# First scan's convolution: four taps on VectorE and GpSimd, or four products with diagonal matrices on TensorE

## The chip, the cores and the metric

The kernel runs on one core of a Trainium2 chip. The metric is the device time of one execution in microseconds; three runs of the kernel before gave 3540.46, 3543.61 and 3543.66 us, a median of 3543.61. All data are float32 unless a line says otherwise.

## The reference, cut to what matters

The input `x` is 32 sequences of 256 tokens with 256 channels. A recurrent block (state space scan) is followed by two transformer layers; the result is added to `x`. Only the front of the recurrent block matters here:

```
xr, gate = split(x @ W_in.T, 2)                 # 512 channels each
xr = xr + t_emb[:, None, :]
xc = conv1d(xr, W_conv, causal, 4 taps, one filter per channel) + b_conv
xc = silu(xc)
xn = layernorm(xc)                              # over the 512 channels
Bm, Cm, dt = split(xn @ W_xproj.T, 3)
h[t] = clip(h[t-1] * Ad[t] + Bd[t] * xn[t], -10, 10)   # scan over 256 tokens
y[t] = Cm[t] . h[t] + D * xn[t];  out = (y * silu(gate)) @ W_out.T
```

The convolution works on each channel by itself: output token t is the sum over k = 0..3 of weight k times input token t - 3 + k. With channels on the 128 partitions, multiplying by one weight per partition is the same as a matrix product with a diagonal 128x128 matrix.

## The kernel before, in words

The 32 sequences are four groups of `GB` = 8. `group_scan(g)` writes the scan of one group: 256 steps in `NCH` = 8 chunks of `CH` = 32 tokens. The 512 inner channels are `NC_` = 4 blocks of 128. For the first group the flag `alone` is true: no transformer work of an earlier group runs beside it. The other groups' scans run beside the transformer layers of the group ahead of them.

All work of a scan is put into numbered slots by `at(slot, function, arguments)`, one slot per step of the recurrence, counted from the scan's first step. `scan_slots` emits the slots in order; a slot's agenda of part 1 comes ahead of its part 2. The framework then orders each engine's instructions itself, by a modelled readiness with the order of emission as the priority (so ScalarE's `tanh` of slot -19 is run ahead of the SiLU of slot -36), allots buffers and sets the semaphores. On the chip every engine follows its fixed order. SyncE issues nearly all loads; its queue is in order too.

Ahead of a chunk that starts at slot s0, block `ch` goes through:

- `project` (slot s0-40+2ch, L401): TensorE multiplies the inputs `xg` by `w_in_sb` into a bank, `ps_in`.
- `conv_in` (s0-38+2ch): GpSimd puts the last three tokens of the chunk before into `xr` (L473, from `carry`); VectorE adds the condition and writes the 32 new tokens of the 8 sequences (L474); GpSimd makes the first tap and the bias, `acc = xr * w0 + b` (L480), and saves the last three tokens (L485). `xr` and `acc` have two buffers each.
- `conv_taps` (s0-37+2ch): VectorE adds three more taps into `acc` (L491).
- `conv_th` (s0-36+2ch): for the first group ScalarE makes `xc = silu(acc)` (L501); for other groups a tanh is used and VectorE finishes in `conv_out` (L511).

Then `raw_sums` (L520, TensorE, slot s0-27) and `norm_turn` (L550, transposes into `tp_x`, s0-26 and s0-22) read `xc`. The statistics follow, and the normed rows go to DRAM (`xnd`); the figures of the recurrence come by `figures_out` (L620, `ps_st`, s0-8) and the lines up to `decays` (s0-5).

The step itself (`step`, L718) is one custom VectorE instruction on 128x512: `h` has eight buffers. It needs a row `xrep`, scaled by ScalarE (`scale_row`, L708). Three of four rows are spread from DRAM by a DMA of 256 KB (`load_rows`, six buffers); for the first group two of every eight rows are spread by TensorE instead (`spread_rows`, L695, `bx`, from `xq`, which `load_skip` loads). `read_out` (L730, `y`) multiplies four steps' `h` on TensorE, each in a column group of its own. `out_turn` (L787, `tz`) and `project_y` (L810, `ps_out`) finish the output.

While the first scan runs, TensorE also makes the projections of the other three groups: 48 calls of `ahead_project` (L428, `ps_a`), six in 32 slots, copied by ScalarE (`xs_a`, L439) and put to DRAM. In the trace one `matmul` of the code shows as two records.

All banks of PSUM come from one pool of eight (`ps_w`, tag "w"). The SBUF pool `ap_` shares buffers by tag; the tags "oT", "hn" and "hT" belong to the transformer layers, which first use them after the first scan. `constants` puts the making of the scan's constants into slots -43 to 68: loads on ScalarE's queue, `td` and `tw` (L303) on TensorE.

Of the kernel before, what the change touches and what calls it, by code (L numbers as in the profile page):

```python
# [10 lines left out]
FP = mybir.dt.float32  # L11
BF = mybir.dt.bfloat16
I32 = mybir.dt.int32
AF = mybir.ActivationFunctionType
ALU = mybir.AluOpType
# [4 lines left out]
P = 128  # L20
# [4 lines left out]
NC_ = DI // P  # L25
NS = 16
GB = 8
CH = 32
# [7 lines left out]
TAPS = 4  # L36
# [16 lines left out]
def bc(ap, axis, n):  # L53

    ap = ap.unsqueeze(axis)
    shape = list(ap.shape)
    shape[axis] = n
    return ap.broadcast_to(shape)
# [15 lines left out]
def kernel(  # L74
# [29 lines left out]
    nc = tc.nc  # L104
# [5 lines left out]
    def loaded(src, shape, name, q=None):  # L110
        t = const.tile(shape, FP, tag=name, name=name)
        (q or nc.scalar).dma_start(out=t, in_=src)
        return t
# [24 lines left out]
    wc_sb = loaded(w_conv, [P, NC_, TAPS], "wc_sb")  # L138
    bconv_sb = loaded(b_conv, [P, NC_], "bconv_sb")
# [5 lines left out]
    ident = const.tile([P, P], FP, tag="ident", name="ident")  # L145
# [73 lines left out]
    for i in range(2):  # L219
        t = const.tile([P, NI * (P + GB)], FP, tag=f"ly{i}", name=f"ly{i}")  # L220
# [3 lines left out]
    def program(ctx, exact):  # L224
        rpool = ctx.enter_context(tc.tile_pool(name="res", bufs=1, reuse_waits="tile"))
        wpool = ctx.enter_context(tc.tile_pool(name="weights", bufs=1, reuse_waits="tile"))
        sp = ctx.enter_context(tc.tile_pool(name="sp", bufs=1, reuse_waits="tile"))
# [4 lines left out]
        ap_ = ctx.enter_context(tc.tile_pool(name="at", bufs=2, reuse_waits="tile"))  # L232
        aw = ctx.enter_context(tc.tile_pool(name="aw", bufs=3, reuse_waits="tile"))
        ps_w = ctx.enter_context(tc.tile_pool(name="psw", bufs=8, space=PSUM, reuse_waits="tile"))

        def bank(pool, tag, name):
            return pool.tile([P, DI], FP, tag=tag, name=name)
# [141 lines left out]
        def group_scan(g):  # L379
# [8 lines left out]
            alone = g == 0  # L388

            agendas = [{}]  # L390
            state = {"p": one}
            ck = [{} for _ in range(NCH)]

            def at(s, what, *args):
                agendas[-1].setdefault(s, []).append(partial(what, *args))
# [66 lines left out]
            def conv_in(c, ch):  # L462
                if ch == 0:
                    ck[c]["carry"] = sm.tile(
                        [P, NC_, GB, TAPS - 1], FP, tag="carry", name="carry"
                    )
                    ck[c]["xc"] = sp.tile([P, NC_, GB * CH], FP, tag="xc", name="xc")
                ps = ck[c].pop(("ps", ch))
                xr = sp.tile([P, GB, TAPS - 1 + CH], FP, tag="xr", name="xr", bufs=2)
                if c == 0:  # L470
                    nc.gpsimd.memset(xr[:, :, 0 : TAPS - 1], 0.0)
                else:
                    nc.gpsimd.tensor_copy(xr[:, :, 0 : TAPS - 1], ck[c - 1]["carry"][:, ch])  # L473
                nc.vector.tensor_add(  # L474
                    xr[:, :, TAPS - 1 :],
                    ps.rearrange("p (b t) -> p b t", b=GB),
                    bc(cond_sb[:, ch, b0 : b0 + GB], 2, CH),
                )
                acc = sp.tile([P, GB, CH], FP, tag="acc", name="acc", bufs=2)
                nc.gpsimd.tensor_scalar(  # L480
                    acc, xr[:, :, 0:CH], wc_sb[:, ch, 0:1], bconv_sb[:, ch : ch + 1],
                    ALU.mult, ALU.add,
                )
                if c < NCH - 1:
                    nc.gpsimd.tensor_copy(ck[c]["carry"][:, ch], xr[:, :, CH:])  # L485
                ck[c]["xr", ch] = xr, acc

            def conv_taps(c, ch):
                xr, acc = ck[c]["xr", ch]
                for k in range(1, TAPS):  # L490
                    nc.vector.scalar_tensor_tensor(  # L491
                        acc, xr[:, :, k : k + CH], wc_sb[:, ch, k : k + 1], acc,
                        ALU.mult, ALU.add,
                    )

            def conv_th(c, ch):
                acc = ck[c]["xr", ch][1]
                if alone:

                    ck[c].pop(("xr", ch))  # L500
                    nc.scalar.activation(  # L501
                        ck[c]["xc"][:, ch], acc.rearrange("p b t -> p (b t)"), AF.Silu
                    )
                    return
                th = sp.tile([P, GB * CH], FP, tag="th", name="th", bufs=2)
                nc.scalar.activation(th, acc.rearrange("p b t -> p (b t)"), AF.Tanh, scale=0.5)
                ck[c]["th", ch] = th
# [173 lines left out]
            def by_tensor(t):  # L681
                return alone and t % (2 * NQ) < XR
# [167 lines left out]
            rep_w = []  # L850
            at(-1, start)
            if alone:
                at(-30, spread_weights)
                constants(at)
            for c in range(NCH):
# [2 lines left out]
            for c in range(NCH):  # L858
                s0 = c * CH
                for hb in range(CH // TB):  # L860
                    s = s0 + hb * TB
                    for i in range(NI):
                        at(s + 4 * i + 5, read_out, c, hb, i)
                    at(s + 21, gated, c, hb)
                    at(s + 25, out_gate, c, hb)
                    at(s + 11, skip, c, hb)
                for ch in range(NC_):
                    at(s0 - 38 + 2 * ch, conv_in, c, ch)
                    at(s0 - 37 + 2 * ch, conv_taps, c, ch)
                    at(s0 - 36 + 2 * ch, conv_th, c, ch)  # L870
                    if not alone:
                        at(s0 - 35 + 2 * ch, conv_out, c, ch)
                for ch, s in enumerate((13, 16, 17, 18)):
                    at(s0 + s + 2, gate_th, c, ch)
                    if not alone:
                        at(s0 + s + 4, gate_out, c, ch)
                at(s0 - 25, raw_copy, c)
                at(s0 - 24, raw_turn, c)
                for j in range(NJ):
                    s = s0 - 26 + 4 * j  # L880
                    at(s + 2, norm_stats, c, j)
                    at(s + 5, norm_shift, c, j)
                    at(s + 5, norm_apply, c, j)
                    at(s + 6, norm_affine, c, j)
                    at(s + 9, norm_out, c, j)
                at(s0 - 11, length, c)
                at(s0 - 9, figures, c)
                at(s0 - 7, figures_in, c)
                at(s0 - 6, decay_th, c)
                at(s0 - 5, decays, c)  # L890
                at(s0 - 4, put_c, c, 0)
                at(s0 + 4, put_c, c, 1)
                for d in range(KM):
                    at(s0 + 45 + 2 * d, copy_y, c, d)
                    at(s0 + 46 + 2 * d, put_y, c, d)
            agendas.append({})
            for c in range(NCH):
                s0 = c * CH
                at(s0 - 43 if alone else s0 + 6, load_x, c)
                if alone:  # L900
                    for ch in range(NC_):
                        at(s0 - 40 + 2 * ch, project, c, ch)
                else:
                    for i in range(2):
                        at(s0 - 44 + 2 * i, load_projected, c, i)
                for ch, s in enumerate((13, 16, 17, 18)):
                    at(s0 + s, project, c, NC_ + ch)
                at(s0 - 27, raw_sums, c)
                for j in range(NJ):
                    at(s0 - 26 + 4 * j, norm_turn, c, j)  # L910
                at(s0 - 8, figures_out, c)
                for t in range(CH):
                    if not by_tensor(t):
                        at(s0 + t - 6, load_rows, c, t)
                    if by_tensor(t) and t % XR == 0:
                        at(s0 + t - 4, spread_rows, c, t)
                    at(s0 + t - 2, scale_row, c, t)
                for hb in range(CH // TB):
                    s = s0 + hb * TB
                    at(s - 9 if alone else s + 7, load_skip, c, hb)  # L920
                    at(s + 23, out_turn, c)
                for d in range(KM):
                    at(s0 + 43 + 2 * d, project_y, c, d)
# [11 lines left out]
        def scan_slots(groups):  # L935


            slots, scans = {}, [group_scan(g) for g in groups]
            for part in range(2):
                for i, agendas in enumerate(scans):  # L940
                    for s, what in agendas[part].items():
                        slots.setdefault(i * S + s, []).extend(what)
            for s in range(min(slots), max(slots) + 1):
                for what in slots.get(s, ()):
                    what()
                yield s
# [617 lines left out]
        s0 = done[0]  # L1564
# [130 lines left out]
```

## Time and profile before

| what | value |
| --- | --- |
| median of three runs | 3543.61 us (3540.46 to 3543.66) |
| profiled execution | 3553.66 us, span 3551.9 us, mean TensorE clock 0.986 |
| busy over the span | PE 97%, DVE 73%, ACT 57%, POOL 46% |
| first step of the first scan (L718) | starts at 59.2 us |
| a chunk of 32 steps in the first scan | 48 to 49 us |
| 0 to 520 us | PE busy 463.5, DVE 419.1, ACT 303.9, POOL 217.5 us |

PE is TensorE (PEld its weight loads), DVE VectorE, ACT ScalarE, POOL GpSimd, SP SyncE. Times in windows are counted from the span's start. A row of the groups has the line, the engine, the operation, output<-inputs, shape and count, then busy microseconds and mean nanoseconds of one, then the idle time of the engine just before these instructions and who ended it. The shares of busy time in the table are means over stages that differ; the first scan is the first 420 us or so.

### The profile page before, as it was taken

What the parts mean: (1) busy time and instruction counts of PE and PEld (TensorE: products, weight loads), DVE (VectorE), ACT (ScalarE), POOL (GpSimd) and SP (SyncE); (2) the same over time, 40 slices, a digit from 0 to 9 for tenths busy, and PEclk for the clock granted to TensorE, in tenths of its full rate; (3) what the DMA queues carried; (4) which work ended last, traced back from release to release, by engine and by line L of the source; (5) the groups of instructions that cost most, each with busy time, mean ns of one, the idle gap of its engine ahead of it and who ended that gap; (6) DMA issues with size and microseconds to landing.
All of it is one profiled execution on the core that took longest, in us unless ns stands there. A gap on an engine that the chain in (4) does not pass through costs nothing.

```text
span 3551.9 us, 57690 instructions
## 1 busy us (share of the span) xinstructions
PE 3441.7 (97%) x20220; PEld 2263.7 (64%) x20220; DVE 2605.5 (73%) x5049; ACT 2037.4 (57%) x3663; POOL 1620.7 (46%) x1587
## 2 busy tenths in 40 slices
PE   7999989999999999999999999999999999999999
PEld 5445335666666666666666666666666777777777
DVE  4888898877878777877787778787777545555563
ACT  3666656656666656666566656666666444444442
POOL 4433455544545445544454556454443333333441
PEclk8999999999999999999999999999999999999999
DMA  6788765534454555544454445544444212011111
GB/s 183 211 219 217 200 174 153 135 113 134 125 143 138 150 144 150 139 121 126 123 144 131 139 147 146 145 115 129 124 138 118 63 37 62 13 31 35 37 28 38
DMA packets 487199, 436.72 MB, mean 123 GB/s; under 512 B 247155, under 2 KB 326516, under 8 KB 486772
## 3 DMA queue, kind: packets, MB, share of 16 engines
q1 hardware_dynamic: 402450, 420.94, 42.0%
q10 hardware_dynamic: 84450, 12.01, 2.1%
q8 instruction: 162, 2.65, 0.3%
q14 instruction: 137, 1.12, 0.1%
HBM read 384.06 MB, written 47.19 MB: 121 GB/s over the span
## 4 chain that ended last, share of the span: by engine, by line
PE 64%; DVE 16%; DMA 7%; ACT 5%; POOL 4%; issue 3%; SPq 1%; ACTq 0%; DVEq 0%; POOLq 0%
PE ps_qkv L991 13%; PE pa L1402 13%; PE po_f L1429 6%; DVE h L718 6%; DMA xrep<-xnd 5%; PE y L730 5%; PE ps_wo L1047 5%; PE ov L1282 4%; PE ps_in L401 3%; PE ps_out L810 3%; PE sc L1227 3%; PE tr_qk L1036 2%; PE rs L1264 2%; ACT xrep L708 2%; DVE acc L491 2%
## 5 line engine op out<-in xcount | busy, mean ns | idle before, releaser
L718 DVE CUSTOM_DVE_ANT_0 h<-h,xrep,lim 128x512 f32<-128x512 f32 x1024 | 931.9, 910 | 215.1 <-ACT xrep L708 166.5
L708 ACT ACTIVATE xrep<-xrep,beta 128x512 f32<-128x512 f32 x960 | 672.5, 720 | 315.7 <-DMA xrep<-xnd 202.4
L991 PE MATMUL ps_qkv<-qkv,res 128*128 128x512 f32 x1536 | 715.2, 601 | 17.2 <-DVE ag L1420 7.2
L1402 PE MATMUL pa<-hT,w 128*128 128x256 f32 (+1 forms) x2816 | 674.5, 382 | 5.4 <-DVE zT L801 5.1
L1402 PEld LDWEIGHTS pa<-hT,w 128*128 128x128 f32 (+1 forms) x2816 | 517.6, 189 | 145.1 <-issue 38.0
L1015 POOL TENSOR_TENSOR rot<-rot,swp 128x512 f32<-128x512 f32 x256 | 349.0, 1363 | 543.7 <-DVE swp L1012 513.0
L991 PEld LDWEIGHTS ps_qkv<-qkv,res 128*128 128x128 f32 x1536 | 282.2, 191 | 299.8 <-issue 242.2
L1021 POOL TENSOR_TENSOR rn<-ss,neg_half 128x8 f32<-128x8 f32 x256 | 461.0, 1801 | 0.0
L1420 DVE SCALAR_TENSOR_TENSOR ag<-pa,b_sb,ag 128x256 f32<-128x256 f32 x320 | 151.9, 475 | 280.0 <-ACT ag L1413 279.7
L730 PE MATMUL y<-h,ly 128*32 128x512 f32 x2048 | 335.8, 606 | 9.8 <-DVE h L718 9.2
L1429 PE MATMUL po_f<-ag,w 128*128 128x256 f32 x1280 | 305.7, 386 | 1.4 <-DVE fo L1440 0.6
L1354 POOL TENSOR_TENSOR rstd<-ve,neg_half 128x2 f32<-128x2 f32 x64 | 46.1, 720 | 555.9 <-DVE ve L1352 555.9
L1429 PEld LDWEIGHTS po_f<-ag,w 128*128 128x128 f32 x1280 | 235.3, 190 | 64.8 <-DVE xc L511 11.7
L1413 ACT ACTIVATE ag<-pa,b_sb 128x256 f32<-128x256 f32 x320 | 149.9, 469 | 217.8 <-PE pa L1402 215.7
L1004 ACT ACTIVATE sq<-ps_qkv,tiny 128x512 f32<-128x512 f32 x256 | 172.4, 685 | 172.2 <-PE ps_qkv L991 143.8
L1047 PE MATMUL ps_wo<-oT,wo 128*128 128x256 f32 x1024 | 236.2, 385 | 14.2 <-DVE oT L1322 11.2
L1047 PEld LDWEIGHTS ps_wo<-oT,wo 128*128 128x128 f32 x1024 | 196.6, 193 | 45.5 <-issue 9.9
L491 DVE SCALAR_TENSOR_TENSOR acc<-xr,wc_sb,acc 128x256 f32<-128x256 f32 x384 | 188.6, 523 | 46.4 <-POOL acc L480 45.9
L1012 DVE TENSOR_TENSOR swp<-ps_qkv,rs_sb 128x256 f32<-128x256 f32 x512 | 191.8, 416 | 29.8 <-POOL rot L1015 29.6
L1007 DVE TENSOR_TENSOR rot<-ps_qkv,rc_sb 128x512 f32<-128x512 f32 x256 | 173.8, 679 | 45.8 <-ACT sq L1004 45.6
L1239 ACT ACTIVATE pT<-sc 128x512 f32<-128x512 f32 x384 | 202.1, 603 | 7.3 <-PE sc L1227 5.5
L1027 DVE SCALAR_TENSOR_TENSOR rot<-rn,rot 128x512 f32<-128x512 f32 x256 | 196.1, 804 | 5.0 <-POOL rn L1021 4.7
(161 smaller groups left out, 5306.9 us busy)
## 6 DMA issues: line engine op xcount, KB each, us to landing
xrep<-xnd SPq DMA_DIRECT2D x960, 256.0 KB
rb<-inv SPq DMA_DIRECT2D x128, 256.0 KB
xnd<-xn SPq DMA_DIRECT2D x64, 256.0 KB
qkv<-in_wqkv_dram SPq DMA_DIRECT2D x24, 512.0 KB
ahead<-xs_a SPq DMA_DIRECT2D x48, 256.0 KB
xp<-ahead SPq DMA_DIRECT2D x48, 256.0 KB
xd<-xnd SPq DMA_DIRECT2D x192, 64.0 KB
w<-in_w_dram SPq DMA_DIRECT2D x80, 128.0 KB
```

What stands on the lines that cost most here:

```text
L491: nc.vector.scalar_tensor_tensor(acc, xr[:, :, k : k + CH], wc_sb[:, ch, k : k + 1], acc, ALU.mult, ALU.add,)
L708: scaled = nc.scalar.activation(bx, ck[c].pop(("bx", t), bx), AF.Copy, scale=ck[c]["beta"][:, t : t + 1])
L718: nc.vector._custom_dve(TENSOR_ADD_SAT, out=h_new, in0=state["h"], in1=bx, s0=ck[c]["lim"][:, 0, t : t + 1], s1=ck[c]["lim"][:, 1, t : t + 1],
L730: nc.tensor.matmul(ck[c]["y", hb][32 * q : 32 * q + 32, :], ly[hb % 2][:, 32 * t : 32 * t + 32], ck[c].pop(("h", hb * TB + t)), start=(i = ...
L991: nc.tensor.matmul(ps, res[b][:, k, t0 : t0 + W], wt["qkv", a][:, k], start=(k == 0), stop=(k == KM - 1),)
L1015: nc.gpsimd.tensor_add(rot, rot, swp)
L1021: nc.gpsimd.tensor_tensor(rn, ss, neg_half, ALU.pow)
L1027: nc.vector.scalar_tensor_tensor(rot, bc(rn, 2, DH), 1e12, rot, ALU.min, ALU.mult)
L1047: nc.tensor.matmul(po[:, d], wt["wo", 0][:, c, d * P : (d + 1) * P], oT[:, c, :], start=(c == 0), stop=(c == NC_ - 1),)
L1239: nc.scalar.activation(p, banks[r], AF.Exp)
L1402: nc.tensor.matmul(dst[x], wt["w1", m][:, k, x], self.h[:, k], start=(k == 0), stop=(k == KM - 1),)
L1429: nc.tensor.matmul(self.po[:, d], wt["w2", 0][:, m, d * P : (d + 1) * P], self.ag[m], start=(m == 0), stop=(m == len(MCH) - 1),)
```

## The change

For the first group only (`alone`), the taps on GpSimd and VectorE are not issued. Sixteen diagonal matrices are made once by ScalarE, an identity scaled by a weight per partition: `taps_diagonal`, slots -41 to -38, in buffers of the tags "oT", "hn" and "hT". `conv_products` (slot s0-37+2ch) lets TensorE multiply four shifted windows of `xr` (128 x 8 x 32) by the four diagonals, summed in one bank, and SiLU reads that bank with the bias as its operand. `conv_in` still makes `xr` and the carry. Other groups are as before.

```diff
@@ -476,14 +476,42 @@
                     ps.rearrange("p (b t) -> p b t", b=GB),
                     bc(cond_sb[:, ch, b0 : b0 + GB], 2, CH),
                 )
-                acc = sp.tile([P, GB, CH], FP, tag="acc", name="acc", bufs=2)
-                nc.gpsimd.tensor_scalar(
-                    acc, xr[:, :, 0:CH], wc_sb[:, ch, 0:1], bconv_sb[:, ch : ch + 1],
-                    ALU.mult, ALU.add,
-                )
+                acc = None
+                if not alone:
+                    acc = sp.tile([P, GB, CH], FP, tag="acc", name="acc", bufs=2)
+                    nc.gpsimd.tensor_scalar(
+                        acc, xr[:, :, 0:CH], wc_sb[:, ch, 0:1], bconv_sb[:, ch : ch + 1],
+                        ALU.mult, ALU.add,
+                    )
                 if c < NCH - 1:
                     nc.gpsimd.tensor_copy(ck[c]["carry"][:, ch], xr[:, :, CH:])
                 ck[c]["xr", ch] = xr, acc
+
+            def taps_diagonal(ch):
+                if ch == 0:
+                    t = ap_.tile([P, 2, TAPS, P], FP, tag="oT", name="taps", bufs=1)
+                    state["taps", 0], state["taps", 1] = t[:, 0], t[:, 1]
+                elif ch > 1:
+                    state["taps", ch] = ap_.tile(
+                        [P, TAPS, P], FP, tag=("hn", "hT")[ch - 2], name="taps", bufs=1
+                    )
+                for k in range(TAPS):
+                    nc.scalar.activation(
+                        state["taps", ch][:, k], ident, AF.Copy, scale=wc_sb[:, ch, k : k + 1]
+                    )
+
+            def conv_products(c, ch):
+                xr, _ = ck[c]["xr", ch]
+                ps = bank(ps_w, "w", "cv")[:, 0 : GB * CH]
+                for k in range(TAPS):
+                    nc.tensor.matmul(
+                        ps.rearrange("p (b t) -> p b t", b=GB),
+                        state["taps", ch][:, k],
+                        xr[:, :, k : k + CH],
+                        start=(k == 0),
+                        stop=(k == TAPS - 1),
+                    )
+                ck[c]["xr", ch] = xr, ps
 
             def conv_taps(c, ch):
                 xr, acc = ck[c]["xr", ch]
@@ -499,7 +527,7 @@
 
                     ck[c].pop(("xr", ch))
                     nc.scalar.activation(
-                        ck[c]["xc"][:, ch], acc.rearrange("p b t -> p (b t)"), AF.Silu
+                        ck[c]["xc"][:, ch], acc, AF.Silu, bias=bconv_sb[:, ch : ch + 1]
                     )
                     return
                 th = sp.tile([P, GB * CH], FP, tag="th", name="th", bufs=2)
@@ -850,6 +878,8 @@
             rep_w = []
             at(-1, start)
             if alone:
+                for ch in range(NC_):
+                    at(-41 + ch, taps_diagonal, ch)
                 at(-30, spread_weights)
                 constants(at)
             for c in range(NCH):
@@ -866,7 +896,8 @@
                     at(s + 11, skip, c, hb)
                 for ch in range(NC_):
                     at(s0 - 38 + 2 * ch, conv_in, c, ch)
-                    at(s0 - 37 + 2 * ch, conv_taps, c, ch)
+                    if not alone:
+                        at(s0 - 37 + 2 * ch, conv_taps, c, ch)
                     at(s0 - 36 + 2 * ch, conv_th, c, ch)
                     if not alone:
                         at(s0 - 35 + 2 * ch, conv_out, c, ch)
@@ -900,6 +931,7 @@
                 if alone:
                     for ch in range(NC_):
                         at(s0 - 40 + 2 * ch, project, c, ch)
+                        at(s0 - 37 + 2 * ch, conv_products, c, ch)
                 else:
                     for i in range(2):
                         at(s0 - 44 + 2 * i, load_projected, c, i)
```

## The prediction

> **What bounds the kernel now.** I read the page first: over the span PE is busy 97%, DVE 73%, and the chain of waits that ended last is 64% PE. That is a mean over unlike stages, and the change touches only the first scan. So I cut that scan out by windows: the stretch before the first recurrence figures (0 to 52 us), and five whole chunks of 32 steps (101.5 to 345 us, 243.5/5 = 48.7 us a chunk; near each edge, some 50 us apart, PE waits for its `bx`).
>
> ```profile
> core 0: us, PE busy (x) PEld busy (x) DVE busy (x) ACT busy (x) POOL busy (x), PEclk, DMA share, GB/s
> 0.00:52.00 52.00, 37.93 (x139) 30.42 (x140) 17.04 (x51) 11.10 (x21) 19.07 (x59) 0.77 0.66 178
> 101.50:345.00 243.50, 230.04 (x1025) 125.52 (x1024) 212.77 (x365) 156.40 (x288) 95.76 (x129) 0.95 0.80 216
> ```
>
> In the five chunks PE is busy 94%, DVE 87%, and the DMA engines 80%: three resources near their ends, PE nearest. Next the costliest groups of that window, for the operations that go and those that the new ones resemble.
>
> ```profile
> L718 DVE CUSTOM_DVE_ANT_0 h<-h,xrep,lim 128x512 f32<-128x512 f32 x161 | 153.9, 956 | 14.0 <-ACT xrep L708 5.9 <-DVE h L718 1.8 <-PE y L730 1.2
> L708 ACT ACTIVATE xrep<-xrep,beta 128x512 f32<-128x512 f32 x120 | 85.7, 716 | 52.4 <-DMA xrep<-xnd 50.4 <-DVE bcd L634 0.7 <-issue 0.6
> L695 PE MATMUL bx<-xq,rep_w 32*128 32x512 f32 x82 | 32.4, 682 | 7.7 <-DMA xq<-xnd 4.8 <-ACT xrep L708 2.8
> L491 DVE SCALAR_TENSOR_TENSOR acc<-xr,wc_sb,acc 128x256 f32<-128x256 f32 x60 | 29.9, 499 | 6.1 <-POOL acc L480 6.1
> L480 POOL TENSOR_SCALAR acc<-xr,wc_sb,bconv_sb 128x256 f32<-128x256 f32 x20 | 19.0, 952 | 41.3 <-DVE xr L474 37.4 <-ACT xs_a L439 1.9 <-ACT xrep L708 1.9
> ```
>
> A chunk has twelve taps of 0.499 us on DVE and four of 0.952 us on POOL. ACT waits 50.4 us for rows, PE only 7.7 us for its own `xq` and ACT. Busy PE is not PE at its peak, so I laid PE's instructions out in order of time and read from one start to the next:
>
> ```profile
> 203.85 1.07 PE L730 MATMUL y<-h,ly 128*32 128x512 f32 x8
> 204.85 1.13 PE L401 MATMUL ps_in<-xg,w_in_sb 128*128 128x256 f32 x4
> 205.91 1.53 PE L730 MATMUL y<-h,ly 128*32 128x512 f32 x6
> 208.24 1.04 PE L730 MATMUL y<-h,ly 128*32 128x512 f32 x2 [0.80 <-DVE h L718]
> 209.22 2.00 PE L428 MATMUL ps_a<-xa,w_in_sb 128*128 128x256 f32 x8
> 211.14 1.13 PE L695 MATMUL bx<-xq,rep_w 32*128 32x512 f32 x4
> 212.20 2.20 PE L730 MATMUL y<-h,ly 128*32 128x512 f32 x6
> 214.33 1.08 PE L520 MATMUL ps_raw<-xc,wx_sb 128*64 128x256 f32 x4
> ```
>
> One `matmul` of the code is two records (four calls of `ahead_project` show as x8). Eight 128x256 records take 1.92 us (209.22 to 211.14): 0.240 us each at the full clock. `y` x8, four column groups side by side, takes 1.00. Where a step is late the group splits: x6 and a later x2 at 0.97, and x6 itself waits (205.91 to 208.24 is 2.33 us, where an undisturbed x6 takes some 1.3).
>
> **PE's own work in a chunk**, from such start-to-start times at full clock and the code's counts: six `ps_a` x8 at 1.92 = 11.5; four `ps_in` x4 at 1.06 and two x8 at 1.83 = 7.9; eight `y` at 1.00 = 8.0; four `bx` at 1.06 = 4.2; `ps_raw` 2.0; `tp_x` 1.0; `tz` 1.0; two `ps_out` at 1.83 = 3.7; `ps_st` 0.5. Sum 39.8 us. Two or three split `y` groups bring it to 42.8. So of 48.7 us PE loses 5.9 to waits and to the slower clock that follows them (the window's mean clock is 0.95), 8.9 if the splits are counted as lost.
>
> **Removed, a chunk:** 12 x 0.499 = 6.0 us of DVE, 4 x 0.952 = 3.8 us of POOL, and some of the stretching of `h` (mean 0.956 us; undisturbed ones in the timeline take 0.80, those beside POOL work 1.2 to 1.7). DVE falls from 42.6 to about 35 busy of 48.7. The hand-over DVE `xr` to POOL `acc` to DVE goes (6.1 us in five chunks). No DMA is added or moved, on SP's, ACT's or POOL's queue.
>
> **Added, a chunk:** 4 channels x 4 products x 2 records = 32 records of 128x256, the shape of `ps_a`: 32 x 0.240 = 7.7 us of PE. I take 0.240, not `ps_in` x4's 0.265 (8.5 us), since eight records run back to back; at the slow clock the same shape takes 0.45 (14.4 us). The weight loads lie under the products, as `ps_a`'s do (190 ns under 240). So PE's work becomes 47.5 without split groups, 50.5 with them.
>
> The Trainium skill's page "TensorE: Matmul & The Clock Gate", section "Back-to-back issue gap", gives 262 cycles, an estimated 0.109 us, for a 256-wide product at full clock; by it the addition would be 3.5 us and the period would fall. The row says 0.240, and the row is of this very shape and type. Its "Perfetto Trace Analysis", section "Identifying the Most-Contended Engine", would judge PE by weight loading, here 125.52/243.5 = 52%: half free, and the change free of cost. The starts on PE contradict that.
>
> **Smaller terms.** SiLU with its bias out of a bank is not in the trace. `xc` out of SBUF takes 0.41 us, `sg` out of a bank with a scattered write 0.659, so between 0 and +1.0 us of ACT a chunk; I take 0.2, under ACT's waits for rows (about 10 us a chunk); without that cover it is on the path. It now waits for PE where it waited for DVE (1.9 us in five chunks); behind it on ACT stand the row scalings, hence the steps. But PE is then at most one slot behind its order and the steps may lie eight `h` buffers ahead, so I price that at 0, at most four products of 1.92 late by a slot (+1.5 a chunk) if that lead is gone. The new wait of PE, products for `xr`, comes two slots (3 us) after the projection, and `xr` takes 0.42 behind a step or two of 0.8: 0; without that lead up to 1.2 a channel. What queues behind it is `y` and `bx`. The bank that is held from product to SiLU is four more on top of some 32 a chunk out of eight banks: 0 to +1. POOL's carry copies for the next `xr` now wait for PE in place of the taps, two channels ahead: 0.
>
> **What of it is lost time filled?** DVE's relief makes the steps early, so the splits and waits for `h` should go: PE's work is then 47.5. What I keep is the wait for `xq` and ACT at the chunk's edge (7.7/5 = 1.5 us) and 1 us of slow clock behind it: 50.0 us. Ends: 47.5 (nothing lost) and 50.5 + 5.9 = 56.4 (nothing absorbed). Against 48.7: +1.3, between -1.2 and +7.7. Chunks 1 to 7 meet this: 7 x 1.3 = +9.
>
> **The start.** Chunk 0's 32 products fall between 12 and 25 us. PE is idle there 3.8 us (0.6 before `td`, 3.16 before `tw`), and from 24 to 51 us one chain of PE work. 7.7 - 3.8 = +4; ends +10.6 (all at the slow clock) and -5 (the products keep the clock up for the `ps_a` after 29 us, which run at 0.39 to 0.47 a record). The 16 diagonals are ACT work of 128x128: between `stat`'s 0.29 and `xc`'s 0.41, 4.6 to 6.6 us in the first 16 us, where ACT is busy 3.2 of 20. Cover: the first `xr` ends at 12.2 us. Without it, or if they queue behind the table load that waits for `wx` until 8.4, the first products wait up to 4 us, inside the ends named.
>
> **Sum:** +9 + 4 = +13 us on the profiled execution (3553.66 us, 1.8 around the span of 3551.9). That is 10.05 above the median 3543.61, 0.28%, much like its spread; I carry the difference over: 3543.6 + 13 = 3557. All later stages keep their work; a longer scan shifts them one to one, as PE is full there.
>
> **Rivals.** (1) *PE's losses stay.* If the waits come from the row transfers (ACT <- DMA `xrep` 50.4 us) and the `xq` at each edge, the 7.7 lie on top: 7 x 7.7 + 4 = +58, 3602. For: `DMA xrep<-xnd` is the largest part of the window's chain. Against: the waits just before split `y` groups name `h`. Chance 0.12. (2) *Steps were the bound* (the other side): DVE loses 6 us a chunk, all of PE's loss is filled, the clock stays full, 7 x -1.2 - 3 = -11, 3532. It decides where PE loses under 0.5 us a chunk and the start does not grow. For: DVE 87% busy, split groups; against: PE's own 47.5 leaves 2%. With it goes a planner that orders the later stages anew, by a few us either way. Chance 0.18. (3) *Nothing to see:* row transfers set the pace (DMA share 0.80, some windows 0.92) and PE's addition is filled; 3544 with 7 either way. Chance 0.22. That the diagonals fail to replace the taps is excluded: no tap is issued for the first group.
>
> **How the numbers follow.** My case, with its own range 3551 to 3580, has 0.48; with rival 1, slower by over 0.2% (7 us, about what a measurement of this kernel can tell from no change) has 0.60, faster 0.18, same 0.22. The range for 8 in 10: down into rival 2 as far as 3536, up to 3588, half way to rival 1.
>
> **What would show it.** Right: no `acc` of L480 and L491 before 380 us; 256 new records of 0.24 us; the window's chunk near 50 us; `y` groups whole; DVE busy near 72% there; PE's idle down to its `xq` waits; first `h` near 63 us against 59.2. Wrong: chunks at 48 us or less (rival 2), or 53 and more with PE still waiting for `bx` and clock below 0.95 (rival 1); or a difference that arises after 450 us.

## The result and the profile after

The changed kernel takes 3586.24 us (median of four, 3581.39 to 3587.88), the kernel before 3543.64 on the same chip: a ratio of 1.0115, 95% interval 1.0102 to 1.0128. It is 42.6 us slower. The sign and the range of the prediction held; the size, +13, was less than a third of it.

Where the time lies is told by one mark, the `MEMSET` of `h` with which the second group's scan begins. It stands at 448.75 us before and at 479.88 after (first line before, second after: start, duration, engine, line): 31.1 us of loss in the first scan.

```profile
448.75 0.48 DVE L838 MEMSET h<- 128x512 f32 x1
479.88 0.48 DVE L866 MEMSET h<- 128x512 f32 x1
```

So the windows are cut there. First after, then before, with the columns of the prediction's windows (start:end, length, busy time and instructions of PE, PEld, DVE, ACT and POOL, granted clock, DMA share, GB/s); the first row is a stretch of the start, the second of after six whole chunks, the last the rest of the program.

```profile
core 0: us, PE busy (x) PEld busy (x) DVE busy (x) ACT busy (x) POOL busy (x), PEclk, DMA share, GB/s
20.00:40.00 20.00, 18.18 (x110) 15.90 (x110) 2.85 (x11) 5.61 (x12) 8.14 (x14) 0.95 0.89 266
92.30:417.00 324.70, 296.05 (x1416) 178.12 (x1417) 205.99 (x367) 192.82 (x349) 89.49 (x125) 0.97 0.74 190
479.90:3584.40 3104.50, 3038.03 (x18530) 2042.63 (x18530) 2246.47 (x4391) 1775.34 (x3181) 1442.49 (x1316) 0.99 0.40 111
```

```profile
20.00:40.00 20.00, 16.84 (x64) 13.53 (x64) 6.23 (x17) 4.47 (x10) 8.52 (x14) 0.63 0.68 207
96.00:387.80 291.80, 275.02 (x1225) 149.86 (x1224) 253.12 (x438) 190.09 (x350) 111.37 (x149) 0.95 0.80 217
448.70:3551.90 3103.20, 3038.00 (x18530) 2044.66 (x18530) 2249.27 (x4392) 1774.58 (x3181) 1442.21 (x1316) 0.99 0.40 111
```

The rest is the same work with the same busy times (18530 PE instructions), 1.3 us longer. The start is shorter: PE has 110 records in place of 64 between 20 and 40 us, the clock there is 0.95 in place of 0.63, and the first `h` comes at 53.42 us in place of 59.23. The chunks are longer: 324.7/6 = 54.1 us. Before, the same measure (from one start of `ps_st`, the product ahead of the recurrence figures, to the one a chunk later) gives 48.6. The six chunks together are 32.9 longer, 5.5 each; the first chunk is 0.3 longer and the stretch from the last of these marks to the `MEMSET` 1.9; the first `ps_st` comes 4.0 earlier (50.88 to 46.85 us): 32.9 + 0.3 + 1.9 - 4.0 = 31.1.

DVE falls to 63% busy (205.99/324.7), PE stands at 91%, and the DMA share falls to 0.74. All three resources that stood near their ends have got room, and the chunk is longer. The costliest groups of these six chunks show what the new work costs:

```profile
L746 DVE CUSTOM_DVE_ANT_0 h<-h,xrep,lim 128x512 f32<-128x512 f32 x192 | 164.5, 857 | 82.3 <-ACT xrep L736 62.5 <-PE y L758 6.2 <-DVE h L746 2.7
L736 ACT ACTIVATE xrep<-xrep,beta 128x512 f32<-128x512 f32 x145 | 104.0, 717 | 124.9 <-DMA xrep<-xnd 111.0 <-DVE h L746 6.3 <-DVE beta L684 3.5
L507 PE MATMUL cv<-xr,taps 128*128 128x256 f32 x192 | 47.8, 391 | 8.8 <-DVE xr L474 8.6 <-ACT xrep L736 0.2
```

The mean `h` falls from 956 (in the prediction's window) to 857 ns. This does not need the relief of DVE and POOL: with the products and all taps kept (*e4_products_added*, below) it is 856. And DVE now waits 82.3 us, ACT 111.0 us for rows. The mean of 391 ns for a product's record overlaps its neighbours', so the price is read from the starts on PE's timeline:

```profile
213.12 1.07 PE L758 MATMUL y<-h,ly 128*32 128x512 f32 x8
214.12 2.00 PE L507 MATMUL cv<-xr,taps 128*128 128x256 f32 x8
215.95 1.02 PE L401 MATMUL ps_in<-xg,w_in_sb 128*128 128x256 f32 x4
216.81 1.89 PE L507 MATMUL cv<-xr,taps 128*128 128x256 f32 x8
218.64 1.07 PE L758 MATMUL y<-h,ly 128*32 128x512 f32 x8
219.91 1.97 PE L507 MATMUL cv<-xr,taps 128*128 128x256 f32 x8 [0.20 <-DVE xr L474]
```

A channel's eight records take 1.83 us (214.12 to 215.95 and 216.81 to 218.64), 0.23 a record, and every `y` is an unsplit x8. Six chunks laid out in this manner, each line's time with the wait behind it, give in us a chunk, before and after:

| line | before | after |
|---|---|---|
| `cv` | 0 | 7.5 |
| `y` | 11.5 | 8.75 |
| `bx` | 6.8 | 5.4 |
| `ps_a` | 12.9 | 11.9 |
| `ps_raw` | 2.0 | 3.0 |
| `ps_in` | 8.95 | 9.6 |
| `tp_x`, `tz`, `ps_st`, `ps_out` | 6.55 | 8.0 |

The products cost 7.5. Three lines give back 5.1 (`y` 2.75, `bx` 1.4, `ps_a` 1.0), and the others take 3.1 more. Where those waits come from is seen in PE's own list for the six chunks (waiter, releaser, us, times, longest):

```profile
PE cv L507 <- DVE xr L474: 8.6, 7, 2.0
PE ps_raw L548 <- ACT xc L529: 5.4, 5, 2.0
```

Neither is among the waits of before, where the largest was `bx` for `xq` (6.8 us in six chunks). In all, PE stands idle for 28.6 us of the six chunks (324.7 - 296.05), where it was 16.8 before (291.8 - 275.02). So the first reading is this: the products displaced some old waits, made two new ones, and cost 5.5 of their 7.5 us.

### The profile page after: what moved, and what is told of

It reads as the page before. It is cut to its first block, busy times and chain, and to the rows that moved or that the text cites. A ratio compares the mean times of both kernels' runs of the same rounds, so it can differ in the third digit from the quotient of the medians.

```text
span 3584.4 us, 58204 instructions
## 1 busy us (share of the span) xinstructions
PE 3466.3 (97%) x20476; PEld 2292.7 (64%) x20476; DVE 2548.9 (71%) x4953; ACT 2047.3 (57%) x3679; POOL 1592.8 (44%) x1555
## 4 chain that ended last, share of the span: by engine, by line
PE 61%; DVE 17%; DMA 8%; ACT 6%; POOL 4%; issue 3%; SPq 1%; ACTq 0%; DVEq 0%; POOLq 0%
PE ps_qkv L1023 13%; PE pa L1434 12%; DVE h L746 7%; DMA xrep<-xnd 6%; PE po_f L1461 6%; PE ps_wo L1079 5%; PE y L758 4%; PE ov L1314 4%; PE sc L1259 3%; PE ps_out L838 3%; PE ps_in L401 2%; PE tr_qk L1068 2%; ACT xrep L736 2%; DVE acc L519 2%; PE rs L1296 2%
## 5 line engine op out<-in xcount | busy, mean ns | idle before, releaser
L746 DVE CUSTOM_DVE_ANT_0 h<-h,xrep,lim 128x512 f32<-128x512 f32 x1024 | 920.7, 899 | 286.4 <-ACT xrep L736 222.9
L758 PE MATMUL y<-h,ly 128*32 128x512 f32 x2048 | 320.3, 608 | 10.2 <-DVE h L746 9.5
L1259 PE MATMUL sc<-qT,kT 64*64 64x192 f32 (+2 forms) x2816 | 187.5, 322 | 0.0
```

The source lines that it names most:

```text
L746: nc.vector._custom_dve(TENSOR_ADD_SAT, out=h_new, in0=state["h"], in1=bx, s0=ck[c]["lim"][:, 0, t : t + 1], s1=ck[c]["lim"][:, 1, t : t + 1],
L758: nc.tensor.matmul(ck[c]["y", hb][32 * q : 32 * q + 32, :], ly[hb % 2][:, 32 * t : 32 * t + 32], ck[c].pop(("h", hb * TB + t)), start=(i = ...
L1259: nc.tensor.matmul(banks[r][k0 : k0 + mk, i, q0:q1], kT[rows, i0 + i, kw * W + k0 : kw * W + k0 + mk], qT[rows, i0 + i, kw * W + q0 : kw * ...
```

## Experiments

Five theories stood at the start. *Work on PE*: PE sets the chunk at nearly constant losses, and the added products are the cause alone. *Relief*: DVE's and POOL's freed time is worth something, or not. *Hand-overs*: the new waits `cv` for `xr` and SiLU for PE make the chunk longer by their place in the order. *SyncE's queue*: it waits longer for the stores of `xs_a` (L444, from `ahead_put`), and rows issued behind them come late. *Rows*: the transfers of rows set the pace. Each ratio is to the kernel before on the same chip.

### How far one execution is to be trusted

*e1_before_again*: the kernel before, unchanged.

> The kernel before once more, for a second profile: its first profiled execution (3553.66 us) was 10 us above the median of its runs (3543.64), so the two traces differ by 32.7 us where the runs differ by 42.6. If the 10 us lie in the first scan, a second profile has first-scan chunks of about 47.5 us instead of 48.7 or a start below 59.2 us. If they lie elsewhere (after the second scan's first step, 3103.2 us in the first profile), the first scan looks the same and the rest is shorter.

One execution took 3556.82 us, beside a median of 3550.49 for this kernel on that chip. Its chunk is 49.4 us, its first `h` at 54.35 (59.23 in the first trace), its clock from 20 to 40 us 0.74, and 3104.6 us remain behind the second `MEMSET`. Two things follow. The early start of the changed kernel is -1 us against this trace and -6 against the first: of the 6, 5 lie between two executions of one kernel. And single executions of the kernels here lie between 7 us below and 10 above their medians, and the chunk of one kernel differed by 0.8 us between two traces: less than that is told by no pair of traces.

### The products without the relief, and the relief without the products

*e4_products_added*: products are made beside all the taps; nobody reads their bank.

```diff
-                if not alone:
+                if True:
                     acc = sp.tile(...)
...
-                ck[c]["xr", ch] = xr, ps
+                ck[c]["unread", ch] = ps
...
-                    if not alone:
-                        at(s0 - 37 + 2 * ch, conv_taps, c, ch)
+                    at(s0 - 37 + 2 * ch, conv_taps, c, ch)
```

> The products alone: diagonals and products as in the changed kernel, but the taps on VectorE and GpSimd stay and feed SiLU; the products' bank is read by nobody. TensorE's addition without VectorE's relief. Work theory: TensorE sets the pace and VectorE's relief is worth little, so within 10 us of the changed kernel, 3580 to 3600. Queue theory and the prediction's rival that steps matter: the relief was worth several us a chunk, so 20 to 60 us slower than the changed kernel, 3606 to 3646.

1.0124 (1.0107 to 1.0141), and a chunk of 54.4 us: the whole loss is there with all the taps kept. The six chunks of this kernel (the same columns), and its longest new wait:

```profile
92.20:418.80 326.60, 295.31 (x1417) 178.54 (x1418) 236.11 (x439) 193.07 (x348) 107.92 (x149) 0.98 0.74 189
PE cv L507 <- DVE xr L474: 17.9, 11, 2.3
```

DVE works 236.11 us instead of 205.99, POOL 107.92 instead of 89.49, and the window is 1.9 us longer, 0.3 a chunk. The `y` groups are whole here too, and the reason can be read from the order of PE's records. Over six chunks this kernel and the changed one have the same 1416 records, named by what they write and read, in the same order, and none of the 48 `y` groups is cut by other work. The two traces of the kernel before have the same 1224 records in one order, and in both 11 of the 48 groups are cut into x6 and x2. So nearly all of the splits were in the order that the framework had written, and are not steps that came late in one execution. And as PE's order is the same with the taps and without, a new order on PE has no part in this pair. SiLU does not wait for PE in this kernel, so that hand-over is not the cause either; PE's wait for `xr` is twice as long, at nearly the same chunk.

*e5_relief_alone*: neither taps nor products, so the convolution's sum is left out.

```diff
-                        at(s0 - 37 + 2 * ch, conv_products, c, ch)
...
-                        ck[c]["xc"][:, ch], acc, AF.Silu, bias=...
+                        ck[c]["xc"][:, ch], xr[:, :, TAPS - 1 :], AF.Silu, bias=...
```

> The relief alone: for the first group neither taps nor products; SiLU reads the newest 32 tokens of xr with the bias, so the convolution's sum is left out. VectorE and GpSimd are relieved as in the change, TensorE gets nothing. Work theory (TensorE's work and what it loses between its pieces set a chunk, and the relief is worth 0.3 us a chunk, as the products alone showed): chunks stay near 48 us, a start some 8 us earlier, ratio to the kernel before 0.996 to 0.999. Rival, the prediction's second (steps were the bound): chunks near 44 us, ratio 0.990 or less.

0.9992 (0.998 to 1.0004), a chunk of 48.9 us. Six chunks:

```profile
81.07:374.32 293.25, 266.27 (x1225) 146.09 (x1225) 215.97 (x367) 190.14 (x347) 97.92 (x125) 0.96 0.83 216
```

DVE falls to 74% (215.97/293.25) and the chunk does not move from the 48.6 and 49.4 of the two traces of before. The first `h` comes at 44.4 us, 10 to 15 earlier than there; of that at most 7 us is seen in the whole time (0.998, the low end). DVE at 87% was not the bound: relieving it is worth nothing that can be told, with the products or without. In this kernel's order 1 of 48 `y` groups is cut, and the chunk is no shorter for it: `y` takes 10.3 us of it, and other lines more than before.

### How much each microsecond on PE costs

*e6_two_products*: two of the four products of each channel.

```diff
-                for k in range(TAPS):
+                for k in range(2, TAPS):
...
-                        start=(k == 0),
+                        start=(k == 2),
```

> The changed kernel with two products in place of four (the two oldest taps are left out): 3.85 us of TensorE a chunk in place of 7.7, all hand-overs as in the change. Work theory: a chunk grows in proportion, by 2.5 to 3 us instead of 5.5, ratio 1.004 to 1.007. Hand-over theory: the waits for xr and the full bank stay, ratio 1.009 or more. Filling theory (the prediction's): what fits into the lost time costs nothing, ratio 0.998 to 1.002.

1.0076 (1.0059 to 1.0093), chunk 51.7 us: 16 records, or 3.85 us of work, give +2.3 to +3.1 against the two traces of before.

*e8_half_ahead*: all products, but each `ahead_project` does half its work, which takes 24 records of the same shape (5.8 us) out of a chunk.

```diff
-                    for k in range(KM):
+                    for k in range(1):
...
-                            start=(k == 0),
-                            stop=(k == KM - 1),
+                            start=True,
+                            stop=True,
```

> The changed kernel with half of the products of ahead_project left out (one of its two input halves): 24 records or 5.8 us of TensorE less a chunk, all in work that no step waits for; copies, stores and loads stay. TensorE's work is 41.7 us a chunk, near the kernel before's 39.8. Work theory: the loss goes with it, chunks of 48 to 50 us, ratio 0.998 to 1.002. Hand-over theory: the products still wait for xr and SiLU for the products, ratio 1.007 or more.

0.9986 (0.9976 to 0.9995), chunk 48.6 us. Every hand-over of the changed kernel is still there, in the same slots, and 5.5 of the loss goes with 5.8 of PE's work that has nothing to do with the convolution. The products do not wait for `xr` at all in this trace, yet PE is idle 26.2 us of the six chunks, nearly the 28.6 of the changed kernel, ahead of other lines.

*e10_bf16_products*: the same products on tiles of half the width.

```diff
-                xr = sp.tile([P, GB, TAPS - 1 + CH], FP, tag="xr", ...)
+                xr = sp.tile([P, GB, TAPS - 1 + CH], BF if alone else FP, tag="xr", ...)
...
-                    t = ap_.tile([P, 2, TAPS, P], FP, tag="oT", ...)
+                    t = ap_.tile([P, 2, TAPS, P], BF, tag="oT", ...)
```

> The change with xr and the diagonals in bf16: 16 records a chunk in place of 32, each about half as long (two bf16 products of 512 columns took 0.52 us from start to start in the transformer layers, so 0.13 for 256): 2.1 us of TensorE a chunk in place of 7.7, with the same hand-overs and the same relief. Work theory, from a growth of 0.7 us for each us of products: +1.5 us a chunk, start 0 to 6 us earlier, ratio 0.999 to 1.003. Hand-over theory: ratio 1.007 or more. Prediction's second rival (steps as the bound): 0.997 or less.

1.0019 (1.0008 to 1.003), chunk 49.75 us. Its timeline:

```profile
195.89 0.61 PE L507 MATMUL cv<-xr,taps 128*128 128x256 bf16 x4
196.43 1.07 PE L758 MATMUL y<-h,ly 128*32 128x512 f32 x8
```

Four products start 0.54 us ahead of `y`: 0.134 each, and one record instead of two; in float32 one product is two records of 0.235. A chunk holds 16 x 0.134 = 2.1 us of them, and it is 0.35 to 1.15 us longer than before. Here the products do wait for `xr`, 8.9 us of the six chunks, as long as in the changed kernel (8.6), and the chunk is 4.4 us shorter. With that the hand-over theory falls: the wait goes neither with the products' presence nor with the chunk. Together, by the work added to PE:

| kernel | PE work added, us a chunk | chunk, us | whole time, ratio |
|---|---|---|---|
| before, two traces | 0 | 48.6, 49.4 | 1 |
| relief alone | 0 | 48.9 | 0.9992 |
| products, half of `ps_a` out | 1.9 | 48.6 | 0.9986 |
| products in bf16 | 2.1 | 49.75 | 1.0019 |
| two products | 3.85 | 51.7 | 1.0076 |
| all products | 7.7 | 54.1 | 1.0115 |
| all products, taps kept | 7.7 | 54.4 | 1.0124 |

Up to some 2 us cost at most 1.15. Above that each us of work costs most of a us, but not a settled share: from half of `ps_a` out to all products 5.5 for 5.8, from two products to four 2.4 for 3.85. A straight line of 0.7 from 48.9 on would fit the last four rows within 0.7 us, and misses half of `ps_a` out by 1.6. Nor is it shown what makes the first part nearly free. The 2.75 that `y` gave back is of that size; but the relief alone has hardly a cut group, adds no work, and has the same chunk, so something else may hold the chunk near 48.6.

### SyncE's queue

After, SyncE's queue waits in the six chunks (same columns as PE's waits):

```profile
SPq L444 <- ACT xs_a L439: 56.3, 23, 7.4
SPq L715 <- DVE h L746: 28.5, 44, 2.0
```

L444 stores `xs_a`; the loads of rows (L715) stand behind it, so the queue could be what makes rows late.

*e2_put_late* and *e3_before_put_late*: the store eight slots later, in the changed kernel and in the one before.

```diff
-                    at(s + 4, ahead_put, u)
+                    at(s + 12, ahead_put, u)
```

> The changed kernel, with the store of the projections made ahead (ahead_put, 48 DMAs on SyncE's queue) eight slots later, so that it stands behind about eight more row loads. Queue theory: with more work on TensorE its ps_a come late, the store waits on SyncE's queue for ScalarE's copy (46.0 us in five chunks, 9.3 before), the row loads queue behind it, ScalarE waits for rows (96.0 against 50.4 us) and TensorE for ScalarE and VectorE. Then the store's wait goes, a chunk falls from about 54.9 to about 50 us, and the kernel gains 25 to 40 us: 3546 to 3561. Work theory: the 7.7 us of products a chunk are simply added and SyncE's waits are only how a full TensorE shows; within 8 us of 3586. Hand-over theory: TensorE's new wait for xr (8.3 us in five chunks) is the loss; unchanged too.

1.0079 (1.0062 to 1.0096), chunk 53.0; L444 still waits 38.6 us.

> The control: the kernel before with the same later store. Its store waits only 9.3 us in five chunks. Queue theory: a small gain, 0 to 10 us, 3534 to 3544. Work theory and hand-over theory: within 5 us of 3544.

0.9992 (0.9982 to 1.0002), chunk 48.55; the wait for the stores is gone from the largest.

*e7_put_on_act*: the changed kernel with the store on ScalarE's queue.

```diff
-                nc.sync.dma_start(out=d, in_=state.pop(("ta", u)))
+                nc.scalar.dma_start(out=d, in_=state.pop(("ta", u)))
```

> The changed kernel with the store of the projections made ahead issued from ScalarE's queue, behind its own copy, so that SyncE never waits for it. Queue theory: SyncE's 46 us of waits in five chunks go, row loads come early, a chunk falls to 50 us, ratio to the kernel before 0.999 to 1.004. Work theory: ratio 1.007 to 1.012, as the later store (1.0079) already showed for a part of that wait.

1.0089 (1.0072 to 1.0106), chunk 52.8. The store no longer stands in SyncE's queue, and another wait has taken its place:

```profile
SPq L715 <- DVE h L746: 76.7, 63, 4.1
```

The queue now waits for a step to free a row's buffer. So the two ways out of the queue give back 1.1 and 1.3 us of the 5.5 in a chunk, little more than the 0.8 between two traces of one kernel (in the whole time 0.0036 of the ratio, with an interval clear of the changed kernel's, and 0.0026, with one that overlaps it). That the rest of SyncE's waiting, for late copies and late steps, is a consequence fits these runs, but none isolates it.

### Rows

*e12_before_more_rows* and *e11_more_rows*: four of eight rows spread by TensorE instead of two, in the kernel before and in the changed one, so that a third of the row loads go.

```diff
-XR = 2
+XR = 4
```

> The control: the kernel before with XR = 4. Row theory: its chunk, with 39.8 us of TensorE's own work in 48.6, falls too, by 2 us or more, ratio 0.997 or less. Otherwise the same or slower: four banks at once for the spread rows.

1.0081 (1.0062 to 1.01), chunk 53.9 us, though the DMA share falls from 0.80 to 0.61.

> The changed kernel with XR = 4: four of every eight rows spread by TensorE instead of two, as four row groups side by side, so eight row loads of 256 KB less a chunk at little or no more of TensorE's time (four calls of spread_rows as before). What is TensorE's remaining loss of 6.6 us a chunk? Row theory: ScalarE's waits for rows (111 us in six chunks) and what follows from them; then with a third of the loads gone a chunk falls by 3 us or more, ratio 1.005 or less. Work theory in its narrow form (waits in TensorE's own hand-overs, the rows being late only because TensorE is): ratio 1.009 to 1.013.

1.0182 (1.0163 to 1.0202), chunk 59.1 us, DMA share 0.54. Fewer loads did not help, but the pair changes more than the loads, for the price of `bx` is not what it seems. From the timeline of the kernel before with four rows:

```profile
172.23 1.14 PE L695 MATMUL bx<-xq,rep_w 32*128 32x512 f32 x8
173.30 1.05 PE L730 MATMUL y<-h,ly 128*32 128x512 f32 x4
```

Four rows take 1.07 us where two took 1.06: by themselves the two added rows are free. But `bx` with the waits behind it takes 60.8 us of six chunks in place of 40.7, 3.4 a chunk more; it now asks for four banks at once. Of the other 1.9 of the 5.3, `y` takes 1.7 (13.2 in place of 11.5). These stalls are mixed with the relief of the rows. What other traces show speaks against rows as the bound: ACT's wait for rows in six chunks is 62.9 us before, but 83.3 in the relief alone and 85.5 with half of `ps_a` out, at the same chunk, and 83.2 in *e11_more_rows*, whose chunk is the longest. It does not go with the chunk. No run takes rows away without adding something else, so they are not excluded.

### The change in the first chunk alone

*e9_first_chunk*: products for chunk 0, taps for the others, to keep the earlier start without the longer chunks.

```diff
-                if not alone:
+                if not (alone and c == 0):
                     acc = sp.tile(...)
...
-                    if not alone:
+                    if not (alone and c == 0):
                         at(s0 - 37 + 2 * ch, conv_taps, c, ch)
...
-                        at(s0 - 37 + 2 * ch, conv_products, c, ch)
+                        if c == 0:
+                            at(s0 - 37 + 2 * ch, conv_products, c, ch)
```

> Products in the first scan's first chunk only; its other seven chunks have the taps of the kernel before. There TensorE is idle for part of the time, and the first step came at 52 to 53 us with products against 54 to 59 us without. Work theory: chunks 1 to 7 as before (48.6 to 49.4 us), the start 0 to 6 us earlier, ratio to the kernel before 0.998 to 1.000. Rival: the products lengthen TensorE's chain in the start too, ratio 1.001 or more.

0.9994 (0.9985 to 1.0004), first `h` at 50.1 us, chunk 48.1: no difference. Over six chunks PE's, DVE's and POOL's orders are here those of the kernel before, record for record, so that 48.1 to 49.4 is what such a chunk varies by. No kernel with all of its work that was run is clearly faster than the kernel before.

## Why the prediction was right and wrong, by its own steps

**The price of the products was right.** 7.7 us a chunk was taken from the row of `ps_a` at 0.240 us a record; 7.5 was measured in place. The Trainium skill's page "TensorE: Matmul & The Clock Gate", section "Back-to-back issue gap", would have made it an estimated 3.5 us and the chunk shorter. The runs contradict it for float32 (0.235 a record, two records a product); in bf16, at 0.134 and one record, the estimate of 0.109 is nearer, though still short.

**The removed work was sized rightly and was worth nothing that shows.** DVE fell to 63% where about 72% was expected of the chunk, because the chunk is longer too. With the taps back (54.4 against 54.1) and with the products out (48.9 against 48.6 and 49.4) it moved the chunk by less than two traces can tell.

**The step that failed is "What of it is lost time filled?"** It let PE's losses fall by two things together: the split `y` groups (42.8 to 39.8 of own work) and, of the other 5.9 us, all but 2.5. The first came true: `y` went from 11.5 to 8.75. The second did not: with whole groups PE's work is 47.5, the chunk 54.1, so 6.6 us are lost where 2.5 were kept. That is 4.1 us too little in each chunk, some 25 us over six; with the loss left at 5.9 the forecast would have been 53.4. The wait that was kept, `bx` for `xq` and ACT, did shrink, from 9.6 us of six chunks to 0.9. But others came: `cv` for `xr`, priced at 0 for its lead of two slots, took 8.6, and `ps_raw` for SiLU, which the prediction did not name, 5.4. By the rows PE's idle time rose from 2.8 us a chunk (3.4 in the second trace) to 4.8; what is lost without showing as idle time, the cut groups aside, fell from about 3.0 to 1.8. Those names do not tell the cause: taking 5.8 us of other work off PE took back the 5.5 while the idle time stayed at 4.4 a chunk, under other names.

**The reason given for the split groups was wrong.** The prediction read them as steps that come late, and expected DVE's relief to mend that. One split in its rows, with `DVE h` beside it, is of that kind; the 11 cut groups of six chunks are in the order of the records, the same in two executions. They went because the framework wrote another order for the changed kernel, and it wrote the same one with all taps on DVE. That this gain was forecast is luck.

**The start had the wrong sign.** +4 was forecast from added work minus idle time; -1 to -6 was seen, as far as the lower end, -5, and past it. The case named there, a clock that stays up for the `ps_a` behind the products, is what the rows show (0.95 against 0.63 and 0.74). The products are not the only way to it: the clock between 20 and 40 us was 0.97 with products and taps, and 1.00 with neither. What goes with the slow clock is idle time of PE at the head of this stretch: `tw` waits there for POOL's `wide`, 3.16 us in the first trace of before and 4.25 in the second, and the kernels with the higher clock have no such wait before 34 us. No run isolates this.

**A further 10 us of the miss is the choice of a reference.** The 10 us that the profiled execution of before lay above its median were carried over to after, whose profiled execution (3586.36) lies at its median. Against the profiled execution the change is +32.7, against the median +42.6. Where those 10 us lay in the first trace stays open.

**The rivals.** Rival 1, PE's losses stay and 7.7 lies on top, is the nearest: its chunk would be 56.4, 2.3 too long, since it did not credit the split groups, and its start was 4 longer. Its mechanism, rows that set the losses, is not shown, and ACT's waits for rows speak against it. Rival 2, the steps as the bound, is disproved by the relief alone. Rival 3, rows that set the pace, would have left the chunk at 48.6. The test that the prediction gave, "chunks at 53 and more with PE still waiting for `bx` and clock below 0.95", came half true: the chunk, but at a clock of 0.97 and with other waits. The time measured is past the end of the prediction's own case (3580), and 2 us inside the range, which had been stretched toward rival 1: that it holds is the width's doing and not the mechanism's.

**What stays open** is why PE loses 6 to 7 us in every chunk. They did not go by less work on DVE (none), by the queue (1.3 at most), or by fewer loads (new stalls in their place). That waits fall on whoever is behind PE's fixed order fits everything seen, but no run isolates it.

## What to carry to other kernels

Busy time that leaves an engine beside the bound is worth nothing until a run with that work simply taken out says otherwise; such a run (here the relief alone) is cheap and answers the question in one number. Where one engine runs an order of many short groups at 94%, do not let added work fill its idle time in a forecast unless the waits that it displaces can be named and new ones excluded: here 5.5 of 7.7 us came through, and the profile gave the remaining waits new names. Before a split group is read as a late step, compare the order of the records in two traces of the same kernel: what is the same in both was written when the kernel was built. Take the forecast from the median and the trace's differences in parts from a second trace of the same kernel, for one execution can lie 10 us off.

## What the runs showed of the chip

A float32 product of 128x256 is two records of 0.235 us, in bf16 one of 0.134: the same sum costs 3.5 times as much of PE in float32. Spreading four rows in four row groups took PE 1.07 us, two rows 1.06. The granted clock between 20 and 40 us differed between two executions of the same kernel (0.63 and 0.74). SiLU with its bias out of a bank took 0.454 us of ACT; out of SBUF it took 0.410 without a bias, and 0.499 with one in the relief alone, where it read the shifted tokens of `xr`. And judging PE by its weight loading, which the Trainium skill's page "Perfetto Trace Analysis", section "Identifying the Most-Contended Engine", names as one of two measures, gives 178.12/324.7 = 55% after and called nearly half of PE free, where beyond some 2 us each added microsecond on PE lengthened the chunk by 0.6 to 0.95.
